# Carries of a selective scan: from its addends to its decays, and one maximum a tile earlier

## The chip, the cores and the metric

The kernel runs on one core of one Trainium2 chip. The metric is the time on the device of one execution, in microseconds (us). The core has a matrix engine (TensorE, PE in the profile), a vector engine (VectorE, DVE), a scalar engine (ScalarE, ACT), a general engine (GpSimd, POOL) and a queue engine that issues most of the DMAs (SyncE, SP). Each engine works its own instructions in order and waits on semaphores for the others. Matrix products land in PSUM; everything else lies in SBUF.

## The reference, cut to what matters

The model has two layers of a mixer and a feed-forward block each. The change lies wholly in the mixer of the second layer, a selective scan over a 64 x 64 image in four directions (B = 4 images, d = 256 channels, N = 16 states a channel, L = 4096 positions):

```python
dts = jnp.einsum('bkrl,kdr->bkdl', dts_r, dt_proj_w)
dt = jax.nn.softplus(dts + dt_proj_b[None, :, :, None])
A = -jnp.exp(A_logs).reshape(K, d, N)
...
def step(h, inp):
    dt_l, u_l, B_l, C_l = inp
    dA = jnp.exp(dt_l[..., None] * A)
    h = h * dA + (dt_l * u_l)[..., None] * B_l[:, :, None, :]
    y = jnp.einsum('bkdn,bkn->bkd', h, C_l)
    return (h, y)
```

Each of the 4 x 256 x 16 states of an image runs through its own recurrence h = h * dA + addend, and y sums h * C over the 16 states.

## The kernel before

`model` runs four parts in turn: attention, a recurrent layer, the selective scan, and the experts. Of the selective scan, `scans` (from L965) is the part concerned; what comes before and after it is not touched.

**Tiles.** The positions of all images in one direction are cut into blocks of T = 125; four blocks are a window of W = 500, and each direction has 33 windows, 132 in all. A tile is one block, four of the 16 states (q) and all 256 channels: 128 partitions, and in the free dimension 2 halves of the channels x 4 states, eight lanes. A lane has T + 1 = 126 places: 125 of data, and one that carries the state in from the block before. So a tile has 1008 elements. A window has 4 groups (q) of 4 tiles, 16 tiles; there are 2112. A "turn" p is one pass of the loop at L1424; the tiles of two groups alternate, so that the tile which goes on from tile p is tile p + 2. The first two directions (k = 2 and 3) run backwards, the others forwards.

**What a tile needs.**
- `decay` (L1194): ScalarE writes exp(dt * A) into a slot of `decays`, a ring of 12 tiles in SBUF. One instruction does one lane of a group's four tiles; a table (`exponentials`, L1375) says in which turn. All other places of `decays` are zero from the start.
- `fill` (L1218): TensorE writes the addends dt * u * B of the tile into `db`, a PSUM tile of two banks with two buffers; eight matmuls (two records each in the trace), and in most tiles four matmuls of zeros onto y between them. It waits until the scan two tiles back has read its buffer.
- `carry_in` (L1257): ScalarE copies the eight last states of tile p - 2 (or of `carries`, or zeros where a sequence begins) into the eight places of `db` that stand ahead of the data. As the decay there is zero, the scan takes the addend as its state and goes on from it. `carry_out` (L1278) keeps the last states of a window's last block in `carries` until the next window.
- `scan` (L1267): one TENSOR_TENSOR_SCAN on VectorE over all 1008 places, into `states`, a ring of 4 tiles.
- `times_c` (L1282): GpSimd multiplies by C into `products`, a ring of 12 tiles.
- `sum_of` (L1297): TensorE sums the products over the states into y, eight matmuls (16 records) in every second turn.

**The preparation of a window.** `project` (L1094) makes a window's dt, dt * u, B and so on. It is a generator whose `yield -18` and the like say in which turn, counted from the window's first tile, the next step is issued. In the tile's numbers of the window that is running, -33 and -17 are both turn 15: two windows are in preparation at once. The steps that matter: x_proj (L1104, -33 and -31) writes `mm`, a PSUM tile; at -22 and -21 ScalarE computes softplus in pieces, GpSimd multiplies `low` (L1139), and ScalarE writes its logarithm over `pts`, which is `mm` again; at -18 and -17 VectorE takes the maximum of the two (L1148), one half of the channels each time; at -17 GpSimd multiplies dt by u (L1150); at -14 and -13 VectorE builds `b_diag` (L1161).

**The order.** It is written out by hand, since the whole runs under `tc.manual_schedule()`; each engine gets its instructions in this order:

```python
for p in range(-BEFORE, max(at) + 12):
    finished(p)
    if p + 1 in at:
        at[p + 1].fill()
        at[p + 1].carry_in()
    if p - 1 in at:
        at[p - 1].carry_out()
    if p in at:
        at[p].scan()
    sums(p)
    if p in at:
        at[p].times_c()
```

After that come the loads of C, the exponentials and the steps of `project` of the turn. `finished` (turn 9 of a window) copies y out on ScalarE (L1331), `add_other` (turn 7, not in the second direction) adds an earlier direction's result to y on TensorE.

Of the kernel before, what the change touches and what calls it, by code (L numbers as in the profile page):

```python
# [19 lines left out]
F32 = mybir.dt.float32  # L20
# [6 lines left out]
P = 128  # L27
B, HW, C = 4, 64, 128
L = HW * HW
CH = 512  # L30
# [5 lines left out]
ND = D // P  # L36
NB, BLOCK = 4, 125
# [22 lines left out]
def backwards(ap):  # L60

    *outer, (step, n) = ap.ap
    return bass.AP(ap.tensor, ap.offset + step * (n - 1), [*outer, [-step, n]])
# [90 lines left out]
def constant(nc, pool, value, name, shape=(P, 1)):  # L154
    t = pool.tile(list(shape), F32, name=name, tag=name)
    nc.vector.memset(t, value)
    return t
# [808 lines left out]
def scans(ctx, tc, a, us, ys, flag):  # L966
# [10 lines left out]
    nc = tc.nc  # L977
    cst = ctx.enter_context(tc.tile_pool(name="sc_c", bufs=1))
    work = ctx.enter_context(tc.tile_pool(name="sc_w", bufs=2))
    dram = ctx.enter_context(tc.tile_pool(name="sc_d", bufs=4, space=DRAM))  # L980
    ps = ctx.enter_context(tc.tile_pool(name="sc_p", bufs=2, space=PSUM))
    T, W, NS, Q = BLOCK, NB * BLOCK, 4, N // 4
# [2 lines left out]
    assert NW * NB == B * JB  # L985
    TILES = Q * NB
    HALF = P // 2
    LANE = 4 * (T + 1)

    RINGS = 12, 4, 12  # L990
    C_RING = 8
    SKIP = CH - LANE

# [5 lines left out]
    for i in range(4):  # L999
        rows = slice(32 * i, 32 * i + 32)  # L1000
        nc.vector.tensor_copy(ident32[rows], ident[rows, rows])
    for i in range(2):
        rows = slice(HALF * i, HALF * i + HALF)
# [18 lines left out]

    decays = cst.tile([P, RINGS[0] * 2 * LANE + 1], F32, name="decays")
    nc.vector.memset(decays, 0.0)
    states = cst.tile([P, RINGS[1] * 2 * LANE], F32, name="states")
    products = cst.tile([P, RINGS[2] * 2 * LANE], F32, name="products")
    slots = {id(ring): n for ring, n in zip((decays, states, products), RINGS)}
    zeros = constant(nc, cst, 0.0, "zeros", (P, P))
    carries = cst.tile([P, ND, Q, 4], F32, name="carries")
    if flag is None:  # L1030
        most = constant(nc, cst, MOST, "most")
    else:
# [4 lines left out]
    def slot_of(ring, t):  # L1037

        n = slots[id(ring)]
        if n % (3 * NB) == 0:  # L1040
            return (t.pair[0].g % (n // NB) * NB + t.nth) * 2 * LANE
        return t.p % n * 2 * LANE

    def window_of(ring, rows, g, n, at, other):

        places = [slot_of(ring, g.tiles[g.v.blocks.index(i)]) + g.h * LANE for i in range(NB)]
        first = ring[rows, places[0] + n * (T + 1) + at :]
        of = bass.AP(
            ring.tensor, first.offset, [first.ap[0], [places[1] - places[0], NB], [1, T]]
        )  # L1050
        return of, other.rearrange("p (i t) -> p i t", i=NB)

    class Window:


        def __init__(self, k, w):
            self.k = k
            self.back = k >= 2
            self.blocks = list(range(NB))[:: -1 if self.back else 1]
            begin = JB - 1 if self.back else 0  # L1060
            self.begins = [i for i in range(NB) if (w * NB + i) % JB == begin]
            self.pieces = []
            for b in range(B):
                first, end = max(w * W, b * LP), min(w * W + W, (b + 1) * LP)
                if first < end:
                    self.pieces.append(
                        (b, slice(first - b * LP, end - b * LP), slice(first - w * W, end - w * W))
                    )

            self.data = slice(0, T) if self.back else slice(1, 1 + T)  # L1070
            self.into = T if self.back else 0
            self.outof = 0 if self.back else T

        def order(self, ap):
            return backwards(ap) if self.back else ap


    STEP = (T - 32) // (NS - 1)
# [15 lines left out]
    def project(v):  # L1094
# [26 lines left out]
        for h, row in enumerate(DT_ROWS):  # L1121
            rows = slice(row, row + R + 1)
# [18 lines left out]
            for h in range(ND):  # L1141
                nc.vector.tensor_max(bound[:, h], pts[:, h], bound[:, h])
        nc.scalar.activation(pts, e, AF.Ln, bias=1.0)
        yield -18
        v.dt = work.tile([P, ND, W], F32, tag="dt", name="dt")
        for h, turn in enumerate((-18, -17)):
            yield turn
            nc.vector.tensor_max(v.dt[:, h], pts[:, h], bound[:, h])  # L1148
        dtu = work.tile([P, ND, W], F32, tag="e", name="dtu", bufs=1)
        nc.gpsimd.tensor_mul(dtu, v.dt, v.u)  # L1150
        yield -15
# [7 lines left out]
        for turn, i in ((-14, 0), (-13, 2)):  # L1159
# [8 lines left out]
            h = i // 2  # L1168
# [4 lines left out]
        for r in range(2):  # L1173
            to, of = (slice(HALF * x, HALF * x + HALF) for x in (r, 1 - r))
# [11 lines left out]
    class Group:  # L1186
# [7 lines left out]
        def decay(self, n):  # L1194
            v = self.v
            at = 4 * self.q + n
            scale = na[:, v.k, self.h, at : at + 1]
            to, dt = window_of(decays, slice(0, P), self, n, 1, v.dt[:, self.h])
            nc.scalar.activation(to, dt, AF.Exp, scale=scale)  # L1199

    class Tile:
# [16 lines left out]
        def fill(self):  # L1218


            self.db = ps.tile([P, 2 * CH], F32, tag="db", name="db")
            y = summed[-1]
            idle = 2 if self.block % 2 else 1
            v = self.v
            for s in range(NS):
                for h in range(ND):
                    first = 32 * ((self.block + 2 * h) % 4)
                    rows = slice(first, first + 32)
                    bank = self.db[:, SKIP + h * LANE :][:, :LANE]
                    at = v.data.start + STEP * s  # L1230
                    b = v.b_other if h else v.b_diag
                    nc.tensor.matmul(  # L1232
                        bank.rearrange("p (n t) -> p n t", n=4)[:, :, at : at + 32],
                        v.dtu[rows, h, s, :],
                        b[rows, s, 4 * self.q : 4 * self.q + 4, :],
                        start=True,
                        stop=True,
                    )
                if y is not None:
                    rows = slice(32 * idle, 32 * idle + 32)  # L1240
                    nc.tensor.matmul(  # L1241
                        y[:, idle // 2, :P], zeros[rows], zeros[rows], start=False, stop=False
                    )

        def edge(self, of, at):

            return of[:, : 2 * LANE].rearrange("p (h n t) -> p h n t", h=ND, t=T + 1)[:, :, :, at]

        def carry(self):

            return carries[:, :, self.q, :]

        def slot(self, ring, shift=0):
            at = slot_of(ring, self) + shift
            return ring[:, at : at + 2 * LANE]

        def carry_in(self):  # L1257

            if self.block in self.v.begins:
                before = zeros[:, : 4 * ND].rearrange("p (h n) -> p h n", h=ND)  # L1260
            elif self.nth:
                before = self.edge(at[self.p - 2].slot(states), self.v.outof)
            else:
                before = self.carry()
            nc.scalar.copy(self.edge(self.db[:, SKIP:], self.v.into), before)  # L1265

        def scan(self):  # L1267
            order = self.v.order
            nc.vector.tensor_tensor_scan(  # L1269
                order(self.slot(states)),  # L1270
                order(self.slot(decays, 1 if self.v.back else 0)),
                order(self.db[:, SKIP:][:, : 2 * LANE]),
                0.0,
                ALU.mult,
                ALU.add,
            )

        def carry_out(self):  # L1278
            if self.nth == NB - 1:
                nc.scalar.copy(self.carry(), self.edge(self.slot(states), self.v.outof))  # L1280

        def times_c(self):  # L1282
            first = c_ring[:, self.c_at :]
            c = bass.AP(
                c_ring.tensor, first.offset, [first.ap[0], [0, ND], [T, 4], [1, T]]
            )
            h, to = (
                self.slot(ring).rearrange("p (l n t) -> p l n t", n=4, t=T + 1)[
                    :, :, :, self.v.data
                ]  # L1290
                for ring in (states, products)
            )
            nc.gpsimd.tensor_mul(to, h, c)  # L1293
# [41 lines left out]
    todo, pairs, at = [], [], {}  # L1335
    for k in (2, 3, 0, 1):
        for w in list(range(NW))[:: -1 if k >= 2 else 1]:
            v = Window(k, w)
            todo.append(v)
            for q in range(Q):  # L1340
                pair = [Group(v, h, q, len(pairs)) for h in range(ND)]
                pairs.append(pair)
                for nth in range(NB):
                    t = Tile(pair[0].start + 2 * nth, pair, nth)
# [5 lines left out]
    with tc.manual_schedule():  # L1350
# [68 lines left out]
        def finished(p):  # L1419
            w, turn = divmod(p - 25, TILES)  # L1420
            if turn == 0 and w in range(len(todo)):
                finish(todo[w])

        for p in range(-BEFORE, max(at) + 12):  # L1424
            finished(p)
            if p + 1 in at:
                at[p + 1].fill()
                at[p + 1].carry_in()
            if p - 1 in at:
                at[p - 1].carry_out()  # L1430
            if p in at:
                at[p].scan()
            sums(p)
            if p in at:
                at[p].times_c()
            if p + 5 in at:
                at[p + 5].load()
            before(p)
            decay(p)
            projections(p)  # L1440
# [380 lines left out]
```

## Time and profile before

| | us |
|---|---|
| median of 3 runs (9727.06 to 9739.29) | 9734.59 |
| the profiled execution, its own time | 9737.04 |
| its span, first to last instruction | 9735.2 |
| first scan starts, last scan starts | 3650.1, 9064.6 |
| VectorE busy | 8335.6 (86%) |
| TensorE busy | 8764.7 (90%) |
| GpSimd busy | 5159.7 (53%) |
| ScalarE busy | 6970.2 (72%) |

The shares of the span mix parts with different limits. Each digit of these rows is the busy share of a fortieth of the span in tenths; the scans are slices 16 to 37:

```profile
PE   7999999999988979999999999999999999999776
DVE  6999999999877219999999999999999999999764
ACT  3888888888755457777777777777777777777321
POOL 0000000000001018999999999999999999999200
```

Three engines are near 90% and more there, so their order among themselves decides. The groups of the page that the change also touches, each with its busy time, the mean of one in ns, and the idle time of its engine just before it:

```profile
L1199 ACT ACTIVATE decays<-dt,a_logs 128x500 f32<-128x500 f32 x4224 | 3014.5, 714 | 86.1
L1232 PE MATMUL db<-b_diag,dtu_t 32*128 32x128 f32 x16896 | 2459.0, 285 | 226.3 <-DVE states L1269 226.2
L1265 ACT COPY db<-states 128x8 f32<-128x8 f32 x1536 | 262.8, 171 | 755.5 <-PE db L1232 742.4
```

A releaser is what ended the wait by the profile; it can itself have been late because of something else. ScalarE stands 755 us before its small copies because they wait for the fills; what is behind them in its queue waits too.

### The profile page before, as it was taken

The page shows a single profiled execution, that of the slowest core. Times are in us where ns is not written, and L with a number is a line of the kernel's source. Part 1 is how long each engine was busy: PE and PEld are TensorE (multiplying, and loading weights), DVE is VectorE, ACT ScalarE, POOL GpSimd, SP SyncE. Part 2 cuts the span into 40 slices and gives each one's busy share as a digit, 9 for nine tenths or more (in the row PEclk, how much of TensorE's full clock was granted, in tenths as well). Part 3 has the DMA queues.
Part 4 walks back from the last instruction along what each step waited for, and adds up shares of the span by engine and source line. Part 5 has one row for each costly group of instructions (what it writes and reads, how often), then busy time and mean ns, then how long its engine had stood idle before and what let it go on. Part 6 is the DMA issues. An engine that isn't in the chain of part 4 may idle for free. (4 is left out here: it accounts for less than half of the span.)

```text
span 9735.2 us, 224869 instructions
## 1 busy us (share of the span) xinstructions
PE 8764.7 (90%) x94770; PEld 4165.3 (43%) x94770; DVE 8335.6 (86%) x5093; ACT 6970.2 (72%) x10894; POOL 5159.7 (53%) x2433
## 2 busy tenths in 40 slices
PE   7999999999988979999999999999999999999776
PEld 3222222222233335555555555555555555555323
DVE  6999999999877219999999999999999999999764
ACT  3888888888755457777777777777777777777321
POOL 0000000000001018999999999999999999999200
PEclk8999999999999979999999999999999999999887
DMA  4000000000012336666665555566665666665634
GB/s 182 16 10 33 8 8 33 10 8 8 9 58 66 118 129 161 163 165 166 167 161 155 147 151 153 153 165 166 165 168 164 165 166 165 167 166 162 223 124 178
DMA packets 530916, 1163.90 MB, mean 120 GB/s; under 512 B 76818, under 2 KB 444506, under 8 KB 502106
## 3 DMA queue, kind: packets, MB, share of 16 engines
q1 hardware_dynamic: 529882, 1149.30, 40.8%
q8 instruction: 748, 12.26, 0.5%
q14 instruction: 286, 2.34, 0.1%
HBM read 828.51 MB, written 182.15 MB: 104 GB/s over the span
## 5 line engine op out<-in xcount | busy, mean ns | idle before, releaser
L1269 DVE TENSOR_TENSOR_SCAN states<-decays,db 128x1008 f32<-128x1008 f32 x2112 | 4671.2, 2243 | 350.6 <-ACT db L1265 311.3
L1293 POOL TENSOR_TENSOR products<-states,c_ring 128x1000 f32<-128x1000 f32 x2112 | 4458.0, 2145 | 383.6 <-PE y L1310 231.8
L1199 ACT ACTIVATE decays<-dt,a_logs 128x500 f32<-128x500 f32 x4224 | 3014.5, 714 | 86.1
L1232 PEld LDWEIGHTS db<-b_diag,dtu_t 32*128 32x128 f32 x16896 | 2077.6, 189 | 1527.7 <-DVE states L1269 917.1
L1232 PE MATMUL db<-b_diag,dtu_t 32*128 32x128 f32 x16896 | 2459.0, 285 | 226.3 <-DVE states L1269 226.2
L1232 PE MATMUL db<-b_other,dtu_t 32*128 32x128 f32 x16896 | 2483.3, 286 | 0.0
L1241 PE MATMUL y<-zeros 32*128 32x128 f32 x14720 | 2151.1, 285 | 0.0
L1232 PEld LDWEIGHTS db<-b_other,dtu_t 32*128 32x128 f32 x16896 | 2074.0, 189 | 0.1
L1310 PE MATMUL y<-products,ident 64*64 64x500 f32 x16896 | 2043.0, 598 | 1.5 <-POOL products L1293 1.5
L334 DVE TENSOR_TENSOR total<-total,ring 128x2048 f32<-128x2048 f32 x768 | 1759.2, 2291 | 67.7 <-DVE total L334 2.8
L1241 PEld LDWEIGHTS y<-zeros 32*128 32x128 f32 x14720 | 1798.2, 188 | 0.0
masks.py:197 POOL MEMSET ident<- 128x128 f32 x6 | 1.2, 205 | 2967.4 <-SPq L180 2675.1
L302 ACT ACTIVATE ring<-sa 128x2048 f32<-128x2048 f32 x640 | 1203.9, 1881 | 453.7 <-PE sa L287 453.6
L311 PE MATMUL av<-ring,v_at 128*32 128x512 f32 x8192 | 1010.0, 599 | 0.1
L1310 PEld LDWEIGHTS y<-products,ident 64*64 64x64 f32 x16896 | 545.7, 133 | 709.3 <-issue 583.5
L1265 ACT COPY db<-states 128x8 f32<-128x8 f32 x1536 | 262.8, 171 | 755.5 <-PE db L1232 742.4
L287 PE MATMUL sa<-q_at,k_at 32*128 32x512 f32 x5120 | 731.8, 641 | 63.0 <-ACT ring L302 37.7
L302 ACT ACTIVATE ring<-sb 128x1536 f32<-128x1536 f32 x512 | 741.2, 1448 | 0.4 <-PE sb L287 0.4
L287 PE MATMUL sb<-q_at,k_at 32*128 32x512 f32 x3072 | 555.6, 615 | 50.9 <-ACT ring L302 50.9
L1104 PE MATMUL mm<-u,w_x 128*128 128x500 f32 x528 | 315.0, 681 | 239.6 <-DVE dt L1148 201.2
L311 PEld LDWEIGHTS av<-ring,v_at 128*32 128x32 f32 x8192 | 210.4, 109 | 701.2 <-issue 676.6
L287 PEld LDWEIGHTS sa<-q_at,k_at 32*128 32x128 f32 x5120 | 200.4, 183 | 618.1 <-ACT ring L302 310.0
(209 smaller groups left out, 8143.4 us busy)
## 6 DMA issues: line engine op xcount, KB each, us to landing
c_ring<-c_rows SPq DMA_DIRECT2D x2112, 250.0 KB, 4.8
b_other<-b_diag SPq DMA_DIRECT2D x264, 512.0 KB, 6.5
weights<-in_w SPq DMA_DIRECT2D x32, 1024.0 KB, 12.9
u<-u_r SPq DMA_DIRECT2D x60, 500.0 KB, 5.8
y_r<-sum SPq DMA_DIRECT2D x60, 500.0 KB, 4.5
u<-u_c SPq DMA_DIRECT2D x60, 500.0 KB, 5.7
y_c<-sum SPq DMA_DIRECT2D x60, 500.0 KB, 4.2
x<-x SPq DMA_DIRECT2D x96, 256.0 KB, 2.6
```

The costliest lines, as they stand in the source:

```text
L287: nc.tensor.matmul(s[:, m, :], k[rows, tokens(t)], q[rows, chunk(chunk_state["c"])], start=True, stop=True,)
L302: nc.scalar.activation(ring[:, lo : lo + n, :], s[:, at : at + n, :], AF.Exp)
L311: nc.tensor.matmul(chunk_state["av"][rows, :], chunk_state["v"][:, t, rows], ring[:, at + i, :], start=t == 0, stop=t == NJ - 1,)
L334: nc.vector.tensor_add(total, total, w)
L1104: nc.tensor.matmul(x_ps[:, :W], w_x[:, h, k, :], v.u[:, h, :], start=h == 0, stop=h == ND - 1)
L1199: nc.scalar.activation(to, dt, AF.Exp, scale=scale)
L1232: nc.tensor.matmul(bank.rearrange("p (n t) -> p n t", n=4)[:, :, at : at + 32], v.dtu[rows, h, s, :], b[rows, s, 4 * self.q : 4 * self.q + ...
L1241: nc.tensor.matmul(y[:, idle // 2, :P], zeros[rows], zeros[rows], start=False, stop=False)
L1265: nc.scalar.copy(self.edge(self.db[:, SKIP:], self.v.into), before)
L1269: nc.vector.tensor_tensor_scan(order(self.slot(states)), order(self.slot(decays, 1 if self.v.back else 0)), order(self.db[:, SKIP:][:, : 2 ...
L1293: nc.gpsimd.tensor_mul(to, h, c)
L1310: nc.tensor.matmul(to, ident[rows, rows], of, start=begins, stop=ends)
```

## The change

A lane gets one place more, S = T + 2 = 127, so a tile has 1016 elements. Its first place (in the direction of the scan) has decay zero and addend one, which makes the state one there; the next has addend zero, and as its decay the state that is carried in, so the state there is one times the carry. The ones and zeros of the addends never change, so they are set once, in two fixed PSUM tiles `dbs` used in turn in place of the pool's two buffers; the fill overwrites only the data. Where the direction turns, the place of the carry moves, and two memsets, one for each slot, make it zero again. `carry` takes the place of `carry_in` and `carry_out`: one ScalarE copy for each tile, from its last states into `decays` of the tile that goes on from it, in the turn after its scan. A window's last block writes straight into the slot of the next window's first tile, and `carries` goes.

In `project` the two maxima are issued in turns -19 and -18 in place of -18 and -17; GpSimd's product of dt and u stays at -17.

```diff
@@ -985,7 +985,8 @@
     assert NW * NB == B * JB
     TILES = Q * NB
     HALF = P // 2
-    LANE = 4 * (T + 1)
+    S = T + 2
+    LANE = 4 * S
 
     RINGS = 12, 4, 12
     C_RING = 8
@@ -1026,7 +1027,11 @@
     products = cst.tile([P, RINGS[2] * 2 * LANE], F32, name="products")
     slots = {id(ring): n for ring, n in zip((decays, states, products), RINGS)}
     zeros = constant(nc, cst, 0.0, "zeros", (P, P))
-    carries = cst.tile([P, ND, Q, 4], F32, name="carries")
+    dbs = [ps.tile([P, 2 * CH], F32, tag=f"db{i}", name=f"db{i}", bufs=1) for i in range(2)]
+    for db in dbs:
+        nc.vector.memset(db[:, SKIP : SKIP + 2 * LANE], 0.0)
+        ones = bass.AP(db.tensor, db.offset + SKIP, [db.ap[0], [S, 4 * ND + 1], [1, 1]])
+        nc.vector.memset(ones, 1.0)
     if flag is None:
         most = constant(nc, cst, MOST, "most")
     else:
@@ -1044,7 +1049,7 @@
     def window_of(ring, rows, g, n, at, other):
 
         places = [slot_of(ring, g.tiles[g.v.blocks.index(i)]) + g.h * LANE for i in range(NB)]
-        first = ring[rows, places[0] + n * (T + 1) + at :]
+        first = ring[rows, places[0] + n * S + at :]
         of = bass.AP(
             ring.tensor, first.offset, [first.ap[0], [places[1] - places[0], NB], [1, T]]
         )
@@ -1067,9 +1072,10 @@
                         (b, slice(first - b * LP, end - b * LP), slice(first - w * W, end - w * W))
                     )
 
-            self.data = slice(0, T) if self.back else slice(1, 1 + T)
-            self.into = T if self.back else 0
-            self.outof = 0 if self.back else T
+            self.data = slice(0, T) if self.back else slice(2, 2 + T)
+            self.into = T + 1 if self.back else 1
+            self.at = 1 if self.back else 2
+            self.outof = 0 if self.back else T + 1
 
         def order(self, ap):
             return backwards(ap) if self.back else ap
@@ -1141,11 +1147,12 @@
             for h in range(ND):
                 nc.vector.tensor_max(bound[:, h], pts[:, h], bound[:, h])
         nc.scalar.activation(pts, e, AF.Ln, bias=1.0)
-        yield -18
+        yield -19
         v.dt = work.tile([P, ND, W], F32, tag="dt", name="dt")
-        for h, turn in enumerate((-18, -17)):
+        for h, turn in enumerate((-19, -18)):
             yield turn
             nc.vector.tensor_max(v.dt[:, h], pts[:, h], bound[:, h])
+        yield -17
         dtu = work.tile([P, ND, W], F32, tag="e", name="dtu", bufs=1)
         nc.gpsimd.tensor_mul(dtu, v.dt, v.u)
         yield -15
@@ -1195,7 +1202,7 @@
             v = self.v
             at = 4 * self.q + n
             scale = na[:, v.k, self.h, at : at + 1]
-            to, dt = window_of(decays, slice(0, P), self, n, 1, v.dt[:, self.h])
+            to, dt = window_of(decays, slice(0, P), self, n, v.at, v.dt[:, self.h])
             nc.scalar.activation(to, dt, AF.Exp, scale=scale)
 
     class Tile:
@@ -1218,19 +1225,21 @@
         def fill(self):
 
 
-            self.db = ps.tile([P, 2 * CH], F32, tag="db", name="db")
+            self.db = dbs[self.p % 2]
             y = summed[-1]
             idle = 2 if self.block % 2 else 1
             v = self.v
+            if self.p - 2 in at and at[self.p - 2].v.back != v.back:
+                nc.vector.memset(self.edge(self.db[:, SKIP:], v.into), 0.0)
             for s in range(NS):
                 for h in range(ND):
                     first = 32 * ((self.block + 2 * h) % 4)
                     rows = slice(first, first + 32)
                     bank = self.db[:, SKIP + h * LANE :][:, :LANE]
-                    at = v.data.start + STEP * s
+                    to = v.at + STEP * s
                     b = v.b_other if h else v.b_diag
                     nc.tensor.matmul(
-                        bank.rearrange("p (n t) -> p n t", n=4)[:, :, at : at + 32],
+                        bank.rearrange("p (n t) -> p n t", n=4)[:, :, to : to + 32],
                         v.dtu[rows, h, s, :],
                         b[rows, s, 4 * self.q : 4 * self.q + 4, :],
                         start=True,
@@ -1244,40 +1253,37 @@
 
         def edge(self, of, at):
 
-            return of[:, : 2 * LANE].rearrange("p (h n t) -> p h n t", h=ND, t=T + 1)[:, :, :, at]
-
-        def carry(self):
-
-            return carries[:, :, self.q, :]
+            return of[:, : 2 * LANE].rearrange("p (h n t) -> p h n t", h=ND, t=S)[:, :, :, at]
 
         def slot(self, ring, shift=0):
             at = slot_of(ring, self) + shift
             return ring[:, at : at + 2 * LANE]
 
-        def carry_in(self):
-
-            if self.block in self.v.begins:
-                before = zeros[:, : 4 * ND].rearrange("p (h n) -> p h n", h=ND)
-            elif self.nth:
-                before = self.edge(at[self.p - 2].slot(states), self.v.outof)
-            else:
-                before = self.carry()
-            nc.scalar.copy(self.edge(self.db[:, SKIP:], self.v.into), before)
-
         def scan(self):
             order = self.v.order
+            shift = 1 if self.v.back else 0
             nc.vector.tensor_tensor_scan(
                 order(self.slot(states)),
-                order(self.slot(decays, 1 if self.v.back else 0)),
-                order(self.db[:, SKIP:][:, : 2 * LANE]),
+                order(self.slot(decays, shift)),
+                order(self.db[:, SKIP + shift :][:, : 2 * LANE]),
                 0.0,
                 ALU.mult,
                 ALU.add,
             )
 
-        def carry_out(self):
-            if self.nth == NB - 1:
-                nc.scalar.copy(self.carry(), self.edge(self.slot(states), self.v.outof))
+        def carry(self):
+
+            if self.nth < NB - 1:
+                later = self.pair[0].tiles[self.nth + 1]
+            elif self.pair[0].g + Q < len(pairs):
+                later = pairs[self.pair[0].g + Q][0].tiles[0]
+            else:
+                return
+            if later.block in later.v.begins:
+                last = zeros[:, : 4 * ND].rearrange("p (h n) -> p h n", h=ND)
+            else:
+                last = self.edge(self.slot(states), self.v.outof)
+            nc.scalar.copy(self.edge(later.slot(decays), later.v.into), last)
 
         def times_c(self):
             first = c_ring[:, self.c_at :]
@@ -1285,7 +1291,7 @@
                 c_ring.tensor, first.offset, [first.ap[0], [0, ND], [T, 4], [1, T]]
             )
             h, to = (
-                self.slot(ring).rearrange("p (l n t) -> p l n t", n=4, t=T + 1)[
+                self.slot(ring).rearrange("p (l n t) -> p l n t", n=4, t=S)[
                     :, :, :, self.v.data
                 ]
                 for ring in (states, products)
@@ -1425,9 +1431,8 @@
             finished(p)
             if p + 1 in at:
                 at[p + 1].fill()
-                at[p + 1].carry_in()
             if p - 1 in at:
-                at[p - 1].carry_out()
+                at[p - 1].carry()
             if p in at:
                 at[p].scan()
             sums(p)
```

## The prediction, made before the change was run

> **What bounds the kernel now.** I read the page first, then the waits by engine, then the timeline of one round of 16 tiles, engine by engine. The stage of the scans runs from 3650 to 9067 us, 5417 of 9735 us, and nothing outside it changes. On the page:
>
> ```profile
> L1269 DVE TENSOR_TENSOR_SCAN states<-decays,db 128x1008 f32<-128x1008 f32 x2112 | 4671.2, 2243 | 350.6 <-ACT db L1265 311.3
> L1293 POOL TENSOR_TENSOR products<-states,c_ring 128x1000 f32<-128x1000 f32 x2112 | 4458.0, 2145 | 383.6 <-PE y L1310 231.8
> ```
>
> VectorE works 86% of this stage in scans alone and waits 350 us before them, put down to the small ScalarE copy at L1265. So at most some 350 us are to be had. In the waits view, VectorE's waits and then TensorE's:
>
> ```profile
> DVE states L1269 <- ACT db L1265: 311.3, 428, 3.2
> PE mm L1104 <- DVE dt L1148: 195.0, 129, 1.6
> ```
>
> The second line happens about once in each of the 132 windows (16 tiles). VectorE's timeline shows where the 350 us lie. I number the tiles of a window 0 to 15; the scan at 7048.51 is tile 10's, because the two maxima (L1148) follow the scans of tiles 14 and 15 and the two b_diag products those of 2 and 3.
>
> ```profile
> 7043.32 4.40 DVE L1269 TENSOR_TENSOR_SCAN states<-decays,db 128x1008 f32<-128x1008 f32 x2 [0.18 <-POOL products L1293]
> 7048.51 11.18 DVE L1269 TENSOR_TENSOR_SCAN states<-decays,db 128x1008 f32<-128x1008 f32 x5 [0.79 <-ACT db L1265]
> 7059.60 0.65 DVE L1148 TENSOR_TENSOR dt<-mm,low 128x500 f32<-128x500 f32 x1
> 7060.17 2.24 DVE L1269 TENSOR_TENSOR_SCAN states<-decays,db 128x1008 f32<-128x1008 f32 x1
> 7062.34 0.65 DVE L1148 TENSOR_TENSOR dt<-mm,low 128x500 f32<-128x500 f32 x1
> 7062.90 2.24 DVE L1269 TENSOR_TENSOR_SCAN states<-decays,db 128x1008 f32<-128x1008 f32 x1
> 7065.55 2.25 DVE L1269 TENSOR_TENSOR_SCAN states<-decays,db 128x1008 f32<-128x1008 f32 x1 [0.41 <-ACT db L1265]
> 7068.50 2.25 DVE L1269 TENSOR_TENSOR_SCAN states<-decays,db 128x1008 f32<-128x1008 f32 x1 [0.69 <-ACT db L1265]
> 7070.67 1.20 DVE L1161 TENSOR_TENSOR b_diag<-mm,ident 128x1024 f32<-128x1024 f32 x1
> 7071.78 2.24 DVE L1269 TENSOR_TENSOR_SCAN states<-decays,db 128x1008 f32<-128x1008 f32 x1
> 7073.94 1.20 DVE L1161 TENSOR_TENSOR b_diag<-mm,ident 128x1024 f32<-128x1024 f32 x1
> 7075.06 8.68 DVE L1269 TENSOR_TENSOR_SCAN states<-decays,db 128x1008 f32<-128x1008 f32 x4
> ```
>
> Starts give the steps: a scan 2.15, a maximum 0.57, a b_diag product 1.12 us. The tiles waited for are 8 (0.18), 10 (0.79), 1 (0.41) and 2 (0.69). GpSimd and TensorE in the same window:
>
> ```profile
> 7047.06 8.40 POOL L1293 TENSOR_TENSOR products<-states,c_ring 128x1000 f32<-128x1000 f32 x4 [1.71 <-PE y L1310]
> 7055.42 2.29 POOL L1139 TENSOR_TENSOR low<-low,e 128x1000 f32<-128x1000 f32 x1
> ```
> ```profile
> 7036.76 0.37 PE L1232 MATMUL db<-b_diag,dtu_t 32*128 32x128 f32 x1 [0.27 <-DVE states L1269]
> ...
> 7063.04 0.69 PE L1104 MATMUL mm<-u,w_x 128*128 128x500 f32 x1 [1.48 <-DVE dt L1148]
> ```
>
> TensorE has no gap from 7036.76 (fill of tile 6) past the fill of tile 10: it sets tiles 8, 10 and 12. Then it stands 1.48 us because the x_proj matmul (L1104) overwrites what the second maximum reads, and the fills of tiles 1 and 2 behind it come late. That is the cause of the waits at tiles 1 and 2, though the page names ScalarE's copy, the last link. In some windows it costs more:
>
> ```profile
> 7303.40:7306.80 3.40, 1.93 (x33) 1.14 (x26) 3.40 (x4) 2.70 (x6) 3.40 (x3) 0.99 0.32 94
> 7306.80:7310.20 3.40, 3.40 (x26) 1.94 (x26) 1.95 (x1) 0.07 (x1) 3.40 (x3) 0.50 0.65 137
> ```
>
> In these lines of the windows view the second field is TensorE's busy time and the third number from the right its granted clock: behind such a gap it is halved for 3.4 us.
>
> [...]
>
> **The change part by part.** I write times from T, the end of tile 4's scan (7036.7), and follow one window.
>
> Longer scans: 8 more elements,[...] the step becomes 2.167. The bounds are 0 and 8 x 2.23 = 18 ns. Products keep 1000 elements.
>
> Carries: the copy no longer follows the fill; it needs only the scan two tiles back. A scan can start 0.04 us after its fill (VectorE's usual delay behind TensorE in other stages of this trace) instead of 0.31 (0.04, the copy's 0.17 and 0.10: fill end 7065.24, copy 7065.28, scan 7065.55). The copy has a whole scan, 2.17 us, to hide in. Its worst place is tile 10, where it stands in ScalarE's queue behind the sum's copy (L1331, 0.97), which waits for TensorE until T+10.24: it ends near T+11.35. The 528 copies to carries (0.2 us each) go, on an engine with idle time. So tile 10 can start at T+11.45 (was 11.81) and tile 12, at TensorE's pace, near 16.05 (was 16.3); tile 13's scan ends at about T+20.4 (was 20.73).
>
> The maximum: the first one now follows tile 13, the second tile 14. The x_proj matmul finds the second one done (TensorE's fill of tile 0 lies between), so the gap of 1.48 us goes, and with it the waits at tiles 1 and 2. But the first maximum reads low, which GpSimd ends at 7055.42 + 2.29 = T+21.01. Before, it came at 7059.60 = T+22.9 with 1.9 us to spare. Now VectorE is there at T+20.4 and must wait 0.65 us; tile 14's scan and all behind it are held. GpSimd can't be earlier: its four products before low begin when TensorE's sums of turn 8 end (7046.94), and TensorE's unbroken run to there starts at T. Whatever the carries gain at tiles 10 and 12 is lost in this wait.
>
> From there VectorE runs unbroken to the next T: first maximum at T+21.05, then 0.57; seven steps of 2.167 (tiles 14, 15, 0 to 4) = 15.17; the second maximum 0.57; two b_diag 2.24. Sum T+39.6. TensorE checked on the way: its fill of tile 2 ends near 30.7 and VectorE comes at 30.9, so tile 2 is the next to be late, by a hair. GpSimd's work is 16 x 2.1 + 2 x 2.3 = 38.2, inside 39.6. A window goes from 40.6 (7048.51 less 7007.92) to 39.6: -0.98 us.
>
> In the second of the four directions nothing is added by add_other and TensorE is earlier: low ends at 5987.69, T = 5967.40, so T+20.3, and the window takes 40.1 (6005.25 less 5965.16). Same sum: 20.35 + 18.6 = 38.95, -1.17 us.
>
> Clock: 132 windows at these lengths give 99 x 40.6 + 33 x 40.1 = 5343 us; the stage takes 5417. Of the 74 us some 5 to 8 are start and end; about 66 are windows of 42.2 or 43.8 us whose TensorE ran at half clock behind the gap at L1104. The largest idle share in any 3.4 us after the change is near 0.95 us (before tiles 0 and 1) against 1.48; gaps of 0.65 and 0.27 close together cost nothing in this trace. I take all 66; the bounds are 0 and 66.
>
> Edits at nothing or near: the memsets of the two slots, 2 us at the start; two memsets where the direction turns; db's two fixed slots wait for the same scan as the two buffers did.
>
> Sum on the profiled execution (9737.0): -97 (99 x 0.98) - 39 (33 x 1.17) - 66 + 2 = 9537. The profiled one is 2.4 above the median of 9734.6; I say 9535.
>
> **Rivals.**
> A, forecast: the wait for low sets the round; 9535. Its own range is 9505 to 9565 (delay from GpSimd to VectorE 0.04 to 0.15 us, the last of the slow clock).
> B: low doesn't hold VectorE, because GpSimd comes earlier to it than I read; 0.65 less in each window, 86 us: 9449. Against it: GpSimd's 1.71 us behind TensorE's sums remain.
> C: the slow clock stays, or TensorE is late at tiles 1 and 2 by about 0.5 us (132 x 0.5 = 66): 9601. For it: the margin at tile 2 is 0.2 us.
> D, slower: GpSimd reaches low one product later (2.1 us) than in this trace, and the moved maximum holds VectorE at tile 13 for 2.75 us. Windows become 41.7 and 41.05, +111 + 31 - 66: 9811. It decides from a delay of 1.5 us (202 us over 132). Against it: low ends at T+21.01 and T+21.02 in the two windows I read.
> E: no change, another wait takes all of it: 9735.
>
> **How the numbers follow.** A 0.60, B 0.10, C 0.20, D 0.06, E 0.04. The range 9445 to 9615 takes in A, B and C. A difference under 0.2% (20 us) can't be told from none here: faster 0.90 (A, B, C), same 0.04 (E), slower 0.06 (D).
>
> **What would show it.** Right: the maximum (the old L1148) has an idle time of about 0.6 us before it, released by low, in every window (some 85 us in all); TensorE's wait before x_proj (195 us) is gone; scans last 2260 ns; no half clock in the scans; windows of 39.6 and 38.95. Wrong: waits before the scans of tiles 1 and 2 that stay, a round nearer 39.0 (B), or over 2 us before the maximum (D).

## The result, and the profile after

The changed kernel takes 9567.81 us in the median of four runs (9564.89 to 9575.03) against 9732.33 us for the kernel before (9727.06 to 9739.29). The ratio is 0.9832, with a 95% interval from 0.9815 to 0.9849. The forecast was 9535 us with a range of 9445 to 9615: the time fell by 165 us where some 200 were forecast.

All of it comes from the scans. In the traces the first one starts at 3648.6 us and the last at 8896.8 (before 3650.1 and 9064.6), so this stage became 166 us shorter. The same two groups of the page, with the number of each, its busy time, the mean of one in ns, and the idle time just before it with its releaser:

```profile
L1265 DVE TENSOR_TENSOR_SCAN states<-decays,db 128x1016 f32<-128x1016 f32 x2112 | 4668.8, 2256 | 100.8 <-ACT decays L1286 60.9
L1299 POOL TENSOR_TENSOR products<-states,c_ring 128x1000 f32<-128x1000 f32 x2112 | 4456.2, 2149 | 219.4 <-PE y L1316 185.3
```

VectorE's idle time before scans fell from 350.6 to 100.8 us, and the mean scan became 13 ns longer for its 8 more elements. A new wait took part of what came free. In the waits of VectorE from 3650 to 9000 us (total, times, longest):

```profile
DVE dt L1154 <- POOL low L1145: 63.7, 129, 0.5
DVE states L1265 <- ACT decays L1286: 60.9, 99, 1.0
DVE states L1265 <- PE db L1241: 35.8, 133, 2.6
```

The first line is the moved maximum, which waits 0.5 us for GpSimd's low in nearly every window. The second comes 99 times, in the windows with add_other, before tile 10. The third is the wait for TensorE's fill, before tile 12 in the lines below. VectorE's timeline of one window, from tile 14 to tile 14 of the next (start, length, what it does, idle time before it; "..." stands for six scans left out):

```profile
7016.65 2.26 DVE L1265 TENSOR_TENSOR_SCAN states<-decays,db 128x1016 f32<-128x1016 f32 x1
7018.82 0.65 DVE L1154 TENSOR_TENSOR dt<-mm,low 128x500 f32<-128x500 f32 x1
7019.39 8.83 DVE L1265 TENSOR_TENSOR_SCAN states<-decays,db 128x1016 f32<-128x1016 f32 x4
7028.16 1.22 DVE L1168 TENSOR_TENSOR b_diag<-mm,ident 128x1024 f32<-128x1024 f32 x1
7029.30 2.26 DVE L1265 TENSOR_TENSOR_SCAN states<-decays,db 128x1016 f32<-128x1016 f32 x1
7031.48 1.20 DVE L1168 TENSOR_TENSOR b_diag<-mm,ident 128x1024 f32<-128x1024 f32 x1
...
7046.36 4.47 DVE L1265 TENSOR_TENSOR_SCAN states<-decays,db 128x1016 f32<-128x1016 f32 x2 [0.62 <-ACT decays L1286]
7051.00 4.43 DVE L1265 TENSOR_TENSOR_SCAN states<-decays,db 128x1016 f32<-128x1016 f32 x2 [0.17 <-PE db L1241]
7055.93 0.68 DVE L1154 TENSOR_TENSOR dt<-mm,low 128x500 f32<-128x500 f32 x1 [0.50 <-POOL low L1145]
7056.53 2.26 DVE L1265 TENSOR_TENSOR_SCAN states<-decays,db 128x1016 f32<-128x1016 f32 x1
```

Tiles 15, 0, 1 and 2 now run in one piece (the third line); before, tiles 1 and 2 waited 0.41 and 0.69 us. The wait before the first maximum is new. It ends with low, in GpSimd's timeline:

```profile
7045.22 8.40 POOL L1299 TENSOR_TENSOR products<-states,c_ring 128x1000 f32<-128x1000 f32 x4 [1.66 <-PE y L1316]
7053.58 2.32 POOL L1145 TENSOR_TENSOR low<-low,e 128x1000 f32<-128x1000 f32 x1
```

Low ends at 7055.90 and the maximum starts at 7055.93. A window is 39.88 us (7046.36 less 7006.48, the same tile a window earlier), before 40.6. TensorE's clock, third number from the right in the windows view, the kernel before first and the changed one second:

```profile
3700.00:6200.00 2500.00, 2302.68 (x31656) 1352.15 (x31650) 2336.78 (x1218) 1957.55 (x3836) 2324.49 (x1095) 0.98 0.60 160
6300.00:8800.00 2500.00, 2312.36 (x31990) 1356.25 (x31984) 2348.03 (x1222) 1968.95 (x3847) 2332.24 (x1100) 0.99 0.61 166
```
```profile
3700.00:6200.00 2500.00, 2350.14 (x32872) 1387.77 (x32874) 2436.37 (x1265) 1980.06 (x3731) 2415.70 (x1139) 1.00 0.62 165
6300.00:8800.00 2500.00, 2359.26 (x32850) 1381.36 (x32844) 2420.31 (x1255) 1962.35 (x3696) 2391.99 (x1130) 1.00 0.62 170
```

Of 32 stretches at half clock between 3700 and 8800 us one is left (at 6274.87). Before, 33 of the windows took 41.6 to 43.8 us; now one of them takes more than 40.4 (41.1).

### The profile page after: what moved, and what is told of

It reads as the page before. It is cut to its first block, busy times and chain, and to the rows that moved or that the text cites. A ratio compares the mean times of both kernels' runs of the same rounds, so it can differ in the third digit from the quotient of the medians.

```text
span 9568.5 us, 222640 instructions
## 1 busy us (share of the span) xinstructions
PE 8704.4 (91%) x94770; PEld 4134.2 (43%) x94770; DVE 8357.7 (87%) x5099; ACT 6855.5 (72%) x10362; POOL 5157.0 (54%) x2433
## 5 line engine op out<-in xcount | busy, mean ns | idle before, releaser
L1265 DVE TENSOR_TENSOR_SCAN states<-decays,db 128x1016 f32<-128x1016 f32 x2112 | 4668.8, 2256 | 100.8 <-ACT decays L1286 60.9
L1241 PEld LDWEIGHTS db<-b_diag,dtu_t 32*128 32x128 f32 x16896 | 2050.9, 187 | 1607.1 <-DVE states L1265 1187.3
L1241 PE MATMUL db<-b_diag,dtu_t 32*128 32x128 f32 x16896 | 2429.4, 283 | 315.2 <-DVE states L1265 309.5
L1241 PE MATMUL db<-b_other,dtu_t 32*128 32x128 f32 x16896 | 2458.3, 284 | 0.0
L1250 PE MATMUL y<-zeros 32*128 32x128 f32 x14720 | 2122.0, 283 | 0.0
L1241 PEld LDWEIGHTS db<-b_other,dtu_t 32*128 32x128 f32 x16896 | 2049.7, 186 | 0.2 <-issue 0.2
L1316 PE MATMUL y<-products,ident 64*64 64x500 f32 x16896 | 2019.7, 592 | 1.2 <-POOL products L1299 1.2
L1250 PEld LDWEIGHTS y<-zeros 32*128 32x128 f32 x14720 | 1771.8, 186 | 0.0
L287 PE MATMUL sa<-q_at,k_at 32*128 32x512 f32 x5120 | 731.8, 641 | 63.3 <-ACT ring L302 41.6
L1286 ACT COPY decays<-states 128x8 f32<-128x8 f32 x2048 | 405.2, 198 | 535.7 <-DVE states L1265 519.4
L330 DVE TENSOR_TENSOR total<-ring 128x2048 f32<-128x2048 f32 x128 | 293.2, 2290 | 141.4 <-ACT ring L302 141.4
```

Of the source, the lines that this page charges most:

```text
L287: nc.tensor.matmul(s[:, m, :], k[rows, tokens(t)], q[rows, chunk(chunk_state["c"])], start=True, stop=True,)
L330: nc.vector.tensor_add(total, chunk_state["first"], w)
L1241: nc.tensor.matmul(bank.rearrange("p (n t) -> p n t", n=4)[:, :, to : to + 32], v.dtu[rows, h, s, :], b[rows, s, 4 * self.q : 4 * self.q + ...
L1250: nc.tensor.matmul(y[:, idle // 2, :P], zeros[rows], zeros[rows], start=False, stop=False)
L1265: nc.vector.tensor_tensor_scan(order(self.slot(states)), order(self.slot(decays, shift)), order(self.db[:, SKIP + shift :][:, : 2 * LANE]) ...
L1286: nc.scalar.copy(self.edge(later.slot(decays), later.v.into), last)
```

## The experiments

Two theories stood against each other. M: the earlier maximum makes the time, because TensorE no longer stands before x_proj; the wait for low then sets the window, and hides what the carries gain. C: the shorter way of the carries makes it (not the C of the prediction's rivals). Each run's ratio is against the kernel before on the same chip (medians 9734.6 to 9741.33 us).

**One part alone.** `max_only` is the kernel before with this:

```diff
-        yield -18
+        yield -19
         v.dt = work.tile([P, ND, W], F32, tag="dt", name="dt")
-        for h, turn in enumerate((-18, -17)):
+        for h, turn in enumerate((-19, -18)):
             yield turn
             nc.vector.tensor_max(v.dt[:, h], pts[:, h], bound[:, h])
+        yield -17
```

> The kernel before with the maximum alone moved to turns -19 and -18; carries stay in the addends. Theory M (the earlier maximum frees TensorE at x_proj, and the wait for low then sets the window, so that the carries' gain is hidden): the window is 39.8 to 40.0 us, half clock gone from the scans, waits of the first maximum for low of about 0.3 us or more; 9565 to 9590 us. Theory C (the shorter way of the carries is the gain): only the slow clock goes, the scans of tiles 1, 2 and 10 still wait for the small copy; 9650 us or more.

Measured: 9567.93 us, ratio 0.9827 (0.9811 to 0.9844), the time of the whole change. Most windows are 39.90 us, and no stretch of the scans runs at half clock. VectorE's timeline from tile 10 to tile 2:

```profile
7007.59 8.90 DVE L1270 TENSOR_TENSOR_SCAN states<-decays,db 128x1008 f32<-128x1008 f32 x4 [0.80 <-ACT db L1266]
7016.83 0.68 DVE L1148 TENSOR_TENSOR dt<-mm,low 128x500 f32<-128x500 f32 x1 [0.34 <-POOL low L1139]
7017.43 2.25 DVE L1270 TENSOR_TENSOR_SCAN states<-decays,db 128x1008 f32<-128x1008 f32 x1
7019.59 0.65 DVE L1148 TENSOR_TENSOR dt<-mm,low 128x500 f32<-128x500 f32 x1
7020.15 6.53 DVE L1270 TENSOR_TENSOR_SCAN states<-decays,db 128x1008 f32<-128x1008 f32 x3
7026.87 2.25 DVE L1270 TENSOR_TENSOR_SCAN states<-decays,db 128x1008 f32<-128x1008 f32 x1 [0.18 <-ACT db L1266]
```

Tile 10 waits 0.80 us as before the change, and the first maximum only 0.34 in place of 0.50: what VectorE saves at tile 10 when the carries move, it spends waiting for the same low. So once the maximum is moved, the carries add nothing here: theory C is out for the change as it stands.

`carry_only` is the changed kernel with these lines of `project` as before.

> The changed kernel with the maximum back at turns -18 and -17; carries in the decays. Theory M: TensorE still stands some 1.4 us before x_proj and the fills of tiles 1 and 2 come late; the window is about 40.1 us and the half clock stays in some windows; 9670 to 9725 us. Theory C: 9570 to 9620 us.

Measured: 9617.1 us, ratio 0.9882 (0.9865 to 0.9898). That is 53 us below the range of theory M and inside that of theory C, so by its time alone it would speak for C. Its windows show how it comes about. They are 40.3 us (its first maxima start at 7004.11 and 7044.41), 0.3 less than before and 0.2 more than I had worked out for M; in the second direction they are 39.6, 0.5 less than before. Together that is some 45 us. The wait before tile 10 is 0.62 us in place of 0.79, but TensorE still stands before x_proj, for 1.42 us in place of 1.48, and tiles 1 and 2 still come late, now without a copy between the fill and the scan:

```profile
7009.92 2.27 DVE L1264 TENSOR_TENSOR_SCAN states<-decays,db 128x1016 f32<-128x1016 f32 x1 [0.24 <-ACT decays L1285]
7012.85 2.27 DVE L1264 TENSOR_TENSOR_SCAN states<-decays,db 128x1016 f32<-128x1016 f32 x1 [0.66 <-PE db L1240]
```

The first line names a ScalarE copy, but the copy that tile 1 needs had ended at 7007.18; its fill, held behind x_proj, ends at 7009.77. So both waits are for TensorE, as the prediction had it.

The rest is for the most part the clock, some 60 us: I had expected it to stay halved in some windows, and that happens twice in the scans in place of 33 times. (In the trace about 12 us more lie ahead of the scans, which start at 3638.1; nothing was changed there, and over all the traces that start varies from 3638 to 3654.) The stretch of 3.4 us around the stand, in the windows view:

```profile
7005.73:7009.14 3.41, 1.99 (x28) 1.09 (x26) 3.41 (x3) 2.17 (x5) 3.41 (x3) 1.00 0.63 143
```

TensorE is busy for 1.99 us of it, and the clock stays full. In the kernel before it was 1.93 us in the stretch shown in the prediction, and half clock followed. Over the whole stage, 126 of the 129 stands before x_proj are 1.42 to 1.44 us here, and none of them was followed by half clock; of the three longer ones two were (1.50 and 1.59 us). In the kernel before, 128 were 1.47 to 1.63 us, and 33 were followed by half clock. So the gain from the clock isn't the maximum's own: either part brings it. That the few hundredths of a microsecond by which the stand is shorter are the reason fits these counts, but no run changed the stand alone.

Each part alone thus brings most of the gain, and they don't add up: 168 us for the maximum, 119 for the carries, 165 together. The clock can be gained only once, and with the maximum moved the wait for low hides what the carries gain in each window.

**The new wait, taken away and doubled.** `low_early` issues GpSimd's product one turn earlier in the changed kernel:

```diff
-        yield -21
         nc.gpsimd.tensor_mul(bound, bound, e)
+        yield -21
```

> The changed kernel with GpSimd's product low issued one turn earlier (behind the product of tile 10 in place of tile 11). Theory M: low ends 2.1 us earlier, the first maximum waits for nothing, the 0.5 us of each window go and nothing takes their place; window 39.3 to 39.5, 9490 to 9520 us. Rival (another chain is just behind, TensorE's fill of tile 2 or GpSimd itself): 9550 us or more.

Measured: 9490.23 us, ratio 0.9744 (0.9728 to 0.976). Low ends at 7005.88 us there. The first maximum (the second line) has no idle time before it, and a window is 39.27 us (7042.33 less 7003.06):

```profile
7003.06 4.43 DVE L1265 TENSOR_TENSOR_SCAN states<-decays,db 128x1016 f32<-128x1016 f32 x2 [0.17 <-PE db L1241]
7007.41 0.65 DVE L1154 TENSOR_TENSOR dt<-mm,low 128x500 f32<-128x500 f32 x1
...
7037.69 4.47 DVE L1265 TENSOR_TENSOR_SCAN states<-decays,db 128x1016 f32<-128x1016 f32 x2 [0.62 <-ACT decays L1286]
7042.33 4.43 DVE L1265 TENSOR_TENSOR_SCAN states<-decays,db 128x1016 f32<-128x1016 f32 x2 [0.17 <-PE db L1241]
```

0.6 us went from each window, 0.5 of it the wait, and nothing took its place: the wait for low was on the path.

`max_two` has the maximum at turns -20 and -19 in the changed kernel (the lines shown under `max_only`, each of the two turns one earlier still).

> The changed kernel with the maximum one turn earlier still, -20 and -19. Theory M: low comes no earlier, so VectorE waits for it with one scan more behind the wait: 2.6 to 2.8 us before the first maximum, a window of about 42.0 us, 9840 to 9870 us. Rival (the held scan is made up for before the next wait, since low follows VectorE): under 9650 us.

Measured: 10164.12 us, ratio 1.0438 (1.042 to 1.0455), slower than before. The wait is what theory M said, up to 2.7 us in 129 windows; the time is 300 us beyond it. The waits of VectorE and the windows view:

```profile
DVE dt L1154 <- POOL low L1145: 341.7, 129, 2.7
DVE states L1265 <- PE db L1241: 257.2, 350, 2.2
```
```profile
3700.00:9400.00 5700.00, 5088.71 (x67081) 2972.11 (x67080) 4974.25 (x2573) 4033.62 (x7585) 4934.82 (x2313) 0.92 0.56 150
```

The second line was 35.8 us in the changed kernel: now tile 0 waits 1.58 us for its fill and tile 2 another 0.64. With VectorE held, TensorE has to wait for a scan too, for 3.83 us up to a fill at 7012.53 in the window I read. Its clock is halved once in every window, 132 times, mostly for 6.8 us (0.92 on the mean), and the fills behind it are late. Windows are 44.4 us; 42.0 had been worked out without the clock. That the slow clock makes these 2.4 us fits the waits, but no run took it away. So in the changed kernel the first turn of this move is worth 49 us (9617.1 to 9567.81, against 168 in the kernel before), and the next one costs 596 (9567.81 to 10164.12).

**The carries, once low is out of the way.** `low_early_addends` is `max_only` with low one turn earlier: `low_early` without the carries in the decays.

> Carries in the addends as before, the maximum at turns -19 and -18, and low one turn earlier: what low_early is, without the carries in the decays. Theory M (the carries gain some 0.3 us a window at tiles 10, 12 and 2, and the wait for low had hidden it): the window is 39.5 to 39.6 us against 39.27 with the carries in the decays, 9515 to 9540 us. Rival (the carries in the decays are worth nothing in any arrangement, their longer scans eat what they save): 9480 to 9500 us, as low_early.

Measured: 9508.46 us, ratio 0.9761 (0.9748 to 0.9774). That lies between the two expectations, so both missed. The interval overlaps that of `low_early`, which ran on another chip, but the windows of the traces hardly vary: 39.45 us against 39.27. Tiles 8, 10 and 2 wait 0.18, 0.80 and 0.18 us for the copy. The carries are worth 0.18 us a window here (0.21 in the second direction), some 25 us by the windows, while the medians differ by 18; I had expected 0.3 a window.

**TensorE's run before tile 10.** `low_add` is `low_early` with

```diff
-            w, turn = divmod(p - 23, TILES)
+            w, turn = divmod(p - 19, TILES)
             if turn == 0 and w in range(len(todo)):
                 add_other(todo[w])
```

> low_early, and add_other issued at turn 3 of a window in place of turn 7, where TensorE has two idle stretches of 0.55 and 0.29 us. Theory (TensorE's unbroken run from the fill of tile 6 sets tiles 10 and 12, and sums, the sum's copy and low behind it; 1.0 us of it is add_other): the wait of 0.62 us before tile 10 goes in the 99 windows that have add_other; windows of 38.6 to 38.8 us as in the second direction; 9425 to 9445 us. Rival (tile 10 is held by something that stays, as the sum's copy in ScalarE's queue): 9475 us or more.

Measured: 9420.34 us, ratio 0.9669 (0.9656 to 0.9683); again beside `low_add_addends`, 9418.72 us. It beats both kernels, the changed one by 147 us, and is 5 us better than the range I had given. Tiles 4 to 11 run in one piece, with windows of 38.57 us in all four directions:

```profile
7019.94 17.53 DVE L1265 TENSOR_TENSOR_SCAN states<-decays,db 128x1016 f32<-128x1016 f32 x8
7037.64 4.43 DVE L1265 TENSOR_TENSOR_SCAN states<-decays,db 128x1016 f32<-128x1016 f32 x2 [0.17 <-PE db L1241]
7041.99 0.65 DVE L1154 TENSOR_TENSOR dt<-mm,low 128x500 f32<-128x500 f32 x1
```

The wait of 0.62 us before tile 10, put down to ScalarE's copy, went when TensorE got less to do there. In the changed kernel the copy stood behind the copy of y, and that behind TensorE's sums (tile 10 starts at 7006.48):

```profile
7005.29 0.99 ACT L1337 COPY sum<-y 128x1000 f32<-128x1000 f32 x1 [1.48 <-PE y L1316]
7006.18 0.21 ACT L1286 COPY decays<-states 128x8 f32<-128x8 f32 x1
```

The second direction, which has no add_other, confirms it: its windows are 38.6 us in `low_early` and in `low_add` alike.

`low_add_addends` is the same with the carries in the addends.

> low_add with the carries in the addends as before: maximum at -19 and -18, low one turn earlier, add_other at turn 3. Theory M (with TensorE's run shortened, what is left of the carries' worth is a net 0.15 to 0.25 us a window, the saved copy less 0.26 us of longer scans): the window is 38.75 us or a little above, against 38.57 with the carries in the decays; 9435 to 9455 us. Rival (no worth left at all): 9410 to 9425 us, as low_add.

> low_add once more, on the same chip as low_add_addends, so that the two can be set against each other: 9410 to 9430 us under either theory.

Measured on one chip: 9438.59 us, ratio 0.9696 (0.9683 to 0.9709), and 9418.72 us, ratio 0.9672 (0.9659 to 0.9685). The windows are 38.79 and 38.57 us: 0.22 us for the carries, within theory M's 0.15 to 0.25. With the carries in the addends the scan of tile 10 waits for the copy again:

```profile
7004.81 8.75 DVE L1270 TENSOR_TENSOR_SCAN states<-decays,db 128x1008 f32<-128x1008 f32 x4 [0.29 <-ACT db L1266]
```

The two intervals just touch, but each of the five runs of `low_add_again` (9409.15 to 9424.75) is faster than each of the five of `low_add_addends` (9433.76 to 9445.6).

## Why the prediction was right, and where its sizes were off

- **What bounds the stage.** Right: the waits at tiles 1 and 2, named after ScalarE's copy, came from the stand before x_proj. `max_only` takes all of tile 1's wait and all but 0.18 us of tile 2's away with the copies in place; `carry_only` takes the copies away and leaves 0.24 and 0.66 us.
- **The wait for low.** Right in place and nearly in size: 0.65 us forecast, 0.50 measured. From T, here the end of tile 4's scan at 7032.59 + 2.26 = 7034.85, tile 10 starts at T+11.51 (forecast 11.45), tile 12 at 16.15 (16.05), the maximum at 21.08 (21.05), tile 14 at 21.68 (21.62).
- **The carries hidden by it.** Right: 9567.93 us without them, 9567.81 with them, and windows of 39.90 and 39.88.
- **The sum from the maximum to the next T.** This is the term that was mis-sized: it gave a window of 39.6 us, measured 39.88. From the start of tile 14 to T it has seven scans at 2.167, one maximum and two b_diag products, 17.98 us; the trace has 18.20 (7016.65 to 7034.85). 0.09 of the difference is my own slip: T is the end of tile 4's scan, and I counted its step (2.167) where its length (2.26) belongs. Another 0.10 lies between the start of tile 15 and the first b_diag product (8.77 us for four steps, 8.67 forecast), most of it at tile 2, where TensorE's fill is just late. The margin of 0.2 us there had been worked out with 0.04 us from a fill to its scan, and it was 0.14. With the 0.06 up to tile 14 these make 0.25 of the 0.28 us. Over 99 windows that is 28 us, and the windows of the second direction were likewise 39.2 in place of 38.95, 8 us: about the 33 us between forecast and result. (The forecast's own sum for the second direction is 20.35 + 18.55 = 38.90, not 38.95, and 40.1 less 38.95 is 1.15, not 1.17; neither is worth more than 2 us in the total.)
- **The longer scan.** Right: unbroken steps were 2.145 to 2.16 us before and are 2.16 to 2.176, some 16 ns more. The 17 ns in the forecast's step of 2.167 were not shown by the profile of before; in proportion, 8/1008 of its 2243 ns a scan are 18.
- **The clock.** Right in size: all but one of the slow stretches between 3700 and 8800 us are gone. Wrong in tying it to the end of the stand before x_proj: `carry_only` loses nearly all of them too, with 1.42 us of the stand still there. That TensorE's idle share of 3.4 us decides, as the forecast took it, was not shown.
- **Rivals.** B would have needed low earlier; made so, it gave 9490 us. C's late fill of tile 2 was real, but it cost under 0.1 us and not 0.5. D's mechanism is the one of `max_two`, where it does make the kernel slower, by more than I had priced: its clock fell too, which the price had left out.

## What to carry to other kernels

Before an instruction is moved earlier on an engine that works in order (here the first maximum's wait of 0.50 us held tile 14's scan behind it), look up when each of its inputs is made on the path of its own engine: a slack of 1.9 us was used up by one tile's move, and a second tile's move made the kernel slower than it had been. When two edits meet in front of the same wait, time each alone; here the larger edit was worth 119 us alone, nothing on top of the smaller one, and some 20 us again once the wait that the smaller one had brought was taken away. And a wait that the profile puts down to a short copy can be that of something ahead of it: before tile 10 it was what stood before the copy in ScalarE's queue, at tiles 1 and 2 the late fill that the copy followed.

## What the runs showed of the hardware that I had not expected

- **Half clock followed some stands of 1.5 us in a busy array, and others not.** In the kernel before, 17 of 33 stands before x_proj of 1.62 or 1.63 us were followed by half clock, and 16 of 95 of 1.47 or 1.48 us; of the 126 of 1.42 to 1.44 us in `carry_only` none was. TensorE was busy by the records for 1.79 to 1.95 us of the 3.41 us ahead of each half clock in the scans of the kernel before. All 33 changes to half clock there lie on one grid of 3.413 us, to within 0.01 us. Busy time alone didn't decide it: 31 other stretches of that grid with 1.79 to 1.95 us kept the full clock, and one with 2.05 us in `low_early_addends` didn't:

```profile
8753.26:8756.67 3.41, 2.05 (x46) 1.70 (x45) 3.41 (x3) 2.33 (x5) 3.41 (x2) 1.00 0.52 127
8756.67:8760.08 3.41, 3.41 (x28) 1.24 (x25) 3.41 (x2) 2.25 (x4) 3.41 (x3) 0.50 0.57 121
```

- **From a fill to its scan.** A fill's last matmul ends at 7010.98 and the scan starts at 7011.12 in the changed kernel: 0.14 us (the median of 133 such waits), where VectorE stood 0.04 behind TensorE in the other stages of the kernel before (the median of 582 waits). The scan now waits for three engines in place of two (three semaphores in 1587 of the 2112 scans, against two in 1716 before). That this is the reason was not tried, and the ends of matmuls are modelled in the profile.
- **The copy of eight elements.** Into SBUF it takes 198 ns, into PSUM it took 171. In the kernel before it stood between a fill and its scan; now it has a whole scan to hide in.
